# Four graph layers on one core: a shorter DMA tree for row sums, a work list planned with other landing times, and a rearranged head

## The chip, the cores and the metric

The kernel runs on one core of a Trainium2 chip. The metric is the device time of one execution in microseconds (us). Before the change the median of three runs is 1611.81 us (1611.36 to 1612.66).

The engines are named as the profile names them: PE is TensorE's matrix product and PEld its weight load, DVE is VectorE, ACT is ScalarE, POOL is GpSimd, SP is SyncE, which only issues DMAs here. Each engine runs its own list of instructions in order; semaphores hold an instruction until its operands are there.

## The reference

x has 32 graphs of 512 tokens and 128 features; adj is one 512 x 512 matrix of zeros and ones for all graphs. Four layers follow, each of the form x = x + layer(relu(layernorm(x))).

```python
# layer 0: attention-like, one score a[i, j] for each pair of tokens
x_h = elu(h @ Wi + bi)
e = sigmoid(a_tgt[:, :, None] + a_src[:, None, :] + be) * mask   # mask from adj
agg = einsum('bij,bjh->bih', e, x_h)
self_part = x_h * sum(e, axis=-1, keepdims=True)                 # the row sums of e
recv = elu(concat([agg, self_part]) @ Wn + bn)
out = concat([recv, x_h]) @ Wm + bm
# layer 1: five steps of a gated recurrent unit
av = concat([adj @ h, adj @ h])
z = sigmoid(av @ w3.T + ...); r = sigmoid(av @ w4.T + ...)
hv = tanh(av @ w5.T + r * h @ u5.T + ...); h = (1 - z) * h + z * hv
# layer 2: adj @ (h @ weight) + bias
# layer 3: sum over k of adj^k @ h @ weight_1[..., k], k up to 3
```

## The kernel before

**Tiles and number formats.** A graph is one tile of 128 partitions x 512. Graphs go in eight groups of four, since x tiles (kind x) and layer 3 take a group at once. Products with adj run in fp32r with each operand split into two parts, hi and lo (`parts`, line 948: a cast on ACT at L955, a subtraction on DVE at L959). The other products run in fp32. A branch on the values of adj chooses between two arms of the program; for this adj, which holds only zeros and ones, the arm `binary` runs. The branch is taken on the 1x1 tile `other`, which is the count of entries that are neither zero nor one (DVE at L567, four count matmuls at L596, a cast at L601, the branch at L1141).

**What sets the order.** The kernel first describes all its work as operations (`plan.op`), each with an engine, an assumed duration, a due time, its operands, and `result`, the assumed time from its end until others may use what it wrote. For a DMA that is the assumed landing time. A scheduler at build time (`Plan.order`) then walks through its own clock and, for each engine, takes the operation with the earliest turn whose operands are ready and whose buffers are free. What comes out is a fixed list for each engine. Due times are spread by `begin(b)`, 56 us a graph. `nudge` shifts the turns of chosen operations by random amounts from listed seeds: HEAD_NUDGES act on operations due in the first 130 us, TAIL_NUDGES on those due after TAIL. The plan is made up to HEAD (250 us) with the first list; the rest after that. Until 50 us the plan puts matmuls of `ones` with `ones` (L353) where PE would be idle; nothing uses their result.

**Layer 0's row sums.** The scores of a graph are four tiles `es`, one for each quarter of j, built by ACT (tanh, L729) and DVE (mask, L732). They go into PE's product with the messages (L741). Their sums over j come in different ways: for graphs 0 and 1 by matmuls with ones; for graphs 2 to 6 and 28 to 31 by sums of tiles and two fp32r matmuls (L784); and for the 21 graphs 7 to 27 by a tree of DMAs, `totals` (line 645). It works in DRAM tiles of kind m. SP copies es[0] to `half`; POOL's DMAs add es[1], es[2] and es[3] to it; another adds the lower half of its rows to the upper half; SP copies the first 32 of the remaining rows as strips into a small SBUF tile `few` (kind y, 128 x 128); POOL's DMA adds the other 32 to it. DVE transposes blocks of 32 (L659) and reduces (L660). `as_row` (L637, L640) sends the sums through DRAM (kind d) and reads them back as a row for all partitions (f<-d). DVE multiplies (own, L787), ACT puts the saved partial product back into PSUM (L792), and PE adds the product with Wn (L793).

**Other things that go by DMA.** `moved_blocks` and `turned`, `turned_back` transpose a tile by a DVE block transpose (L437), a write to DRAM (m<-f, L439) and a read (f<-m, L450, L469, or four reads at L474 where the order of layer 3 is wanted). The target scores also go through `as_row` from graph 4 on.

**Layer 1's step** is at lines 1000 to 1035: products with u3, adj, w4, w3, w5, u5 on PE (L496, L985), copies on ACT (L485), the sum in front of each gate on DVE (L1010), tanh on ACT (L501), r * h on DVE (L1017), which PE's product with u5 needs.

**The head.** SP and ACT issue the first loads: x of graph 0, then the four adj tiles on ACT's queue, x of graphs 1 to 3, then weights. PE transposes adj (L581), ACT casts it to fp32r (L589, L590). `layernorm` (line 519) takes moments on DVE (L528 to L531), the power -1/2 on POOL (L533), and then either scaling with relu on ACT (L542) or `normed` on DVE (L548, four pieces of 128 x 128; relu follows later, in the cast after the transpose). Behind the branch PE squares adj for layer 3 (L941, 16 matmuls, cast by ACT at L945), permutes its columns with `swap` (L973), and starts graphs 0 to 3.

Of the kernel before, what the change touches and what calls it, by code (L numbers as in the profile page):

```python
# [15 lines left out]
ALU = mybir.AluOpType  # L16
# [7 lines left out]
HEAD, TAIL = 250.0, 1500.0  # L24
HEAD_NUDGES = (7300007, 7300273, 7300133, 7300137, 7300212, 7300214, 7300262, 7300277, 35000194, 7300312, 7300318,
    7300325, 7300868, 7300483, 7300904, 7300717, 7300556, 7300600, 7300611, 7300613, 7300637,
    7300638, 7300675, 7300698, 35000259, 7300709, 7300722, 7300785, 35000013, 7300805, 35000212,
    7300852, 7300896, 35000078, 7300914, 7300921, 35000204, 35000148, 35000027, 35000249, 35000045,
    35000210, 35000052, 35000053, 35000077, 35000088, 35000089, 35000097, 35000105, 35000109,
    35000112, 35000115, 35000120, 35000122, 35000126, 35000131, 35000173, 35000144, 35000159,  # L30
    35000196, 35000203, 35000206, 35000211, 35000219, 35000232, 35000236, 35000250, 35000254,
    35000255, 35000256, 35000257, 35000258, 35000264)
TAIL_NUDGES = ()
# [220 lines left out]
def tile_four_graph_layers(  # L254
# [36 lines left out]
    BRANCH, FILL = 9.0, 50.0  # L291
    MARGIN = 10.0
    FIRST = 4
# [4 lines left out]
    A_LANDS = (2.9, 3.15, 3.4, 3.65)  # L298
# [4 lines left out]
    slots = {"x": 5, "f": 36, "q": 4, "s": 10, "d": 6, "y": 3, "m": 10, "b": 8}  # L303
# [9 lines left out]
    def buffers(pool, kind, n, shape, dt=F32):  # L313
# [7 lines left out]
        "y": buffers(pool, "y", slots["y"], [P, P]),  # L321
# [67 lines left out]
    load_graph(0, -10, 2.45)  # L389
    A_nat = [Val("f") for _ in range(NC)]  # L390
    for ic, v in enumerate(A_nat):
        load(v, adj.rearrange("(p c) n -> c p n", c=NC)[ic], -9.5, 0.45, earliest=0.3, result=A_LANDS[ic], eng="ACT")
    load_graph(1, -8.5, 2.9, 3.0)
    Wi_sb = load_const(Wi, [P, P], "Wi_sb", -8.2, earliest=3.0, result=2.7)
    load_graph(2, -8, 2.9, 3.0)
    load_graph(3, -7.5, 3.1, 3.0)
# [38 lines left out]
    def moved_blocks(src, due, us, view_out, view_in):  # L435
        blocks, moved = Val("f"), Val("m")
        op("DVE", us, due, lambda: nc.vector.transpose(view_out(at(blocks)), view_in(at(src))),  # L437
           [src], [blocks])
        op("SP", T_DMA, due, lambda: nc.sync.dma_start(at(moved), at(blocks)),  # L439
           [blocks], [moved], result=2.6)  # L440
        return moved
# [19 lines left out]
    def turned_back(src, due, in_order=False):  # L461
# [15 lines left out]
        op("SP", (4 if in_order else 1) * T_DMA, due, carry, [moved], [t], result=3.8)  # L477
# [41 lines left out]
    def layernorm(b, due, relu=True, earliest=0.0):  # L519
# [26 lines left out]
        def normed():  # L546
            for c in range(NC):
                nc.vector.tensor_scalar(  # L548
                    at(h)[:, ts(c, P)], at(X[b])[:, c, :], mean()[:, c : c + 1],
                    stat(SCALE)[:, c : c + 1], op0=ALU.subtract, op1=ALU.mult)  # L550
        if relu:
            op("ACT", 1.56, due, scale, [X[b], s], [h])
        else:
            op("DVE", 1.03, due, normed, [X[b], s], [h])
# [9 lines left out]
    n_odd = const("n_odd", [P, NC])  # L564
    for ic in range(NC):
# [3 lines left out]
            op0=ALU.is_gt, op1=ALU.not_equal, accum_out=at(n_odd)[:, ic : ic + 1]),  # L569
            [A_nat[ic]], [odd, n_odd], two=True)  # L570
# [23 lines left out]
    def count():  # L594
        for jc in range(NC):
            nc.tensor.matmul(  # L596
                at(p_odd)[:1, :1], at(n_odd)[:, jc : jc + 1], at(ones)[:, :1],
                start=jc == 0, stop=jc == NC - 1,
            )
    op("PE", 0.3, -1, count, [n_odd, ones], [p_odd])  # L600
# [30 lines left out]
    def as_row(columns, part, d, keep):  # L631
# [10 lines left out]
        op("SP", T_DMA, d, read, [row], [t], keep=keep, result=5.0)  # L642
        return t

    def totals(es, d):

        half, few, turned_few, columns = Val("m"), Val("y"), Val("y"), Val("s")
        def strip(k):
            return at(half)[ts(k, 32), :].rearrange("j (q i) -> q j i", q=4)
        def added(to, of, val):  # L650
            op("POOL", 1.0, d, lambda: nc.gpsimd.dma_start(to(), of(), accum_op=ALU.add),
               [*val, val[-1]], [val[-1]], two=False, result=4.6)
        op("SP", T_DMA, d, lambda: nc.sync.dma_start(at(half), at(es[0])), [es[0]], [half], result=2.6)
        for e in es[1:]:
            added(lambda: at(half), lambda e=e: at(e), [e, half])
        added(lambda: at(half)[: P // 2, :], lambda: at(half)[P // 2 :, :], [half])
        op("SP", T_DMA, d, lambda: nc.sync.dma_start(at(few), strip(0)), [half], [few], result=2.6)
        added(lambda: at(few), lambda: strip(1), [half, few])
        op("DVE", 0.25, d, lambda: nc.vector.transpose(at(turned_few), at(few)), [few], [turned_few])  # L659
        op("DVE", 0.25, d, lambda: nc.vector.tensor_reduce(  # L660
            at(columns)[:, :NC], at(turned_few).rearrange("p (b j) -> p b j", j=32),
            axis=mybir.AxisListType.X, op=ALU.add), [turned_few], [columns])
# [56 lines left out]
    def aggregated(b, begun, due):  # L719
# [43 lines left out]
        else:  # L763
# [13 lines left out]
            high, low, ps = Val("q"), Val("q"), Val("b")  # L777
# [36 lines left out]
    def entry(b):  # L814
        h = layernorm(b, begin(b), relu=b >= FIRST, earliest=begin(b) - 12.0 if b < G else 0.0)
# [17 lines left out]
    def arm(binary):  # L833
        with ExitStack() as stack:
# [15 lines left out]
            order = plan.order(end=HEAD)  # L850
# [3 lines left out]
    def list_rest(binary, pool):  # L854
        for v in crossing:
# [19 lines left out]
        for b in range(G):  # L875
            aggregated(b, begun[b], begin(b))

        n = 20 if binary else 16
        places["r"] = buffers(pool, "r", n, [P, 512], F32R if binary else F32)
        plan.free["r"] = [(0.0, i) for i in range(n)]  # L880
        PARTS = 2 if binary else 1
# [304 lines left out]
```

## Time and profile before

| what | value |
| --- | --- |
| median of 3 runs | 1611.81 us |
| the profiled execution | 1614.92 us |
| its span, first to last instruction | 1613.1 us |
| mean granted PE clock | 0.999 |
| PE busy | 1594.4 us (99%) |
| DVE busy | 1407.0 us (87%) |
| ACT busy | 1134.0 us (70%) |
| POOL busy | 282.5 us (18%) |
| mean share of the 16 DMA engines | 35.2% (q1, from SP and ACT), 12.3% (q0, from POOL) |
| landing f<-d, median | 5.6 us |
| landing m<-f from SP, from POOL | 2.4 us, 4.3 us |
| landing y<-m from POOL | 4.7 us |

A line of the views gives engine, source line, operation, and the tiles as written<-read with buffer numbers left out. In the view of waits, a line names the waiting instruction, then what released it, the sum of idle time, how often, and the longest. In a timeline, the first number is the start in us, the second the length of the merged piece, and what stands in brackets is the engine's idle time before it and what ended it. The span of the profiled execution is 1.8 us below its own time, and that time is 3.1 us above the median of the runs.

One fp32 matmul has two records in the profile, one fp32r matmul has one.

### The profile page before, as it was taken

To read this page: it belongs to the slowest core of one execution; us is meant where nothing else is said; L and a number is where in the kernel's file an instruction comes from. 1 tells how busy PE (TensorE), PEld (TensorE's weight loads), DVE (VectorE), ACT (ScalarE), POOL (GpSimd) and SP (SyncE) were. 2 spreads that over 40 slices of the span, in tenths; PEclk is the share of its full clock that TensorE was granted. 3 is DMA by queue.
4 is the path that set the end of the run, shared out by engine and by line. 5 is a ranking of instruction groups with operands and counts; after the bars stand their busy time and mean duration, and the time that the engine had idled before them with its cause. 6 is when DMAs were issued, how large, how long until landed. Compare 5 with 4: busy or idle time off the path is not lost. (4 is left out here: it accounts for less than half of the span.)

```text
span 1613.1 us, 21201 instructions
## 1 busy us (share of the span) xinstructions
PE 1594.4 (99%) x6285; PEld 1017.6 (63%) x6285; DVE 1407.0 (87%) x3356; ACT 1134.0 (70%) x2146; POOL 282.5 (18%) x286
## 2 busy tenths in 40 slices
PE   9999999999999999999999999999999999999998
PEld 6655555656666566666566665665666665656688
DVE  8899999989988899888989889888998888888772
ACT  7877767877776777766767678767787767666561
POOL 4121112202221122111122111221211111100010
PEclk9999999999999999999999999999999999999999
DMA  4364544554564555555555554555555344423221
GB/s 129 79 152 123 143 133 127 131 137 113 142 147 115 142 142 138 126 134 132 132 136 133 149 127 124 146 137 130 149 135 128 98 132 122 113 79 92 85 60 55
DMA packets 301281, 199.46 MB, mean 124 GB/s; under 512 B 89492, under 2 KB 249876, under 8 KB 300820
## 3 DMA queue, kind: packets, MB, share of 16 engines
q1 hardware_dynamic: 274708, 169.16, 35.2%
q0 software_dynamic: 24288, 27.01, 12.3%
q10 hardware_dynamic: 2160, 1.84, 0.3%
q8 instruction: 52, 0.85, 0.2%
q14 instruction: 73, 0.60, 0.1%
HBM read 93.79 MB, written 98.45 MB: 119 GB/s over the span
## 5 line engine op out<-in xcount | busy, mean ns | idle before, releaser
L485 ACT COPY f<-b 128x512 f32<-128x512 f32 x409 | 234.8, 584 | 157.8 <-PE b L985 109.1
L985 PE MATMUL b<-AQ,r 128*128 128x512 f32 x1024 | 303.9, 439 | 0.0
L533 POOL TENSOR_TENSOR s<-s,nhalf 128x4 f32<-128x4 f32 x128 | 153.6, 1200 | 624.8 <-DVE s L531 564.1
L985 PEld LDWEIGHTS b<-AQ,r 128*128 128x128 f32 x1024 | 192.4, 188 | 89.5 <-issue 43.6
L1010 DVE TENSOR_TENSOR f<-f,b 128x512 f32<-128x512 f32 x320 | 212.7, 677 | 33.0 <-PE b L496 26.2
L985 PE MATMUL b<-adj_r,r 128*128 128x512 f32 x768 | 225.4, 436 | 0.0
L437 DVE STREAM_TRANSPOSE f<-f 128x512 f32<-128x512 f32 x246 | 207.0, 846 | 18.7 <-ACT f L542 17.5
L542 ACT ACTIVATE f<-x,s 128x128 f32<-128x128 f32 x496 | 203.9, 486 | 26.1 <-DVE s L537 25.6
L985 PEld LDWEIGHTS b<-adj_r,r 128*128 128x128 f32 x768 | 144.6, 189 | 62.0 <-issue 26.8
L501 ACT ACTIVATE f<-f,b4w 128x512 f32<-128x512 f32 x160 | 115.3, 721 | 89.8 <-DVE f L1010 89.2
L959 DVE TENSOR_TENSOR r<-f,r 128x512 fp32r<-128x512 f32 x224 | 152.1, 683 | 20.2 <-ACT r L955 19.1
L496 PE MATMUL b<-f,u5T 128*128 128x512 f32 x320 | 163.3, 594 | 3.7 <-DVE f L1017 3.6
L955 ACT CAST r<-f 128x512 fp32r<-128x512 f32 x224 | 137.2, 619 | 42.3 <-DMA f<-m 38.1
L496 PE MATMUL b<-f,w4T 128*128 128x512 f32 x320 | 163.4, 593 | 0.0
L496 PE MATMUL b<-f,w3T 128*128 128x512 f32 x320 | 163.0, 592 | 0.0
L496 PE MATMUL b<-f,u3T 128*128 128x512 f32 x320 | 162.9, 594 | 0.0
L496 PE MATMUL b<-f,w5T 128*128 128x512 f32 x320 | 162.7, 592 | 0.0
L501 ACT ACTIVATE f<-f,b3w 128x512 f32<-128x512 f32 x160 | 115.1, 720 | 40.3 <-DVE f L1010 39.4
L501 ACT ACTIVATE f<-b,b5w 128x512 f32<-128x512 f32 x160 | 109.3, 684 | 36.9 <-PE b L496 36.1
L1060 PEld LDWEIGHTS b<-V,f 128*128 128x128 f32 x1024 | 122.4, 192 | 15.7 <-issue 14.1
L1027 DVE TENSOR_TENSOR f<-f,f 128x512 f32<-128x512 f32 x160 | 108.6, 680 | 22.4 <-ACT f L501 20.1
L1060 PE MATMUL b<-V,f 128*128 128x128 f32 x1024 | 123.7, 275 | 0.0
(121 smaller groups left out, 2339.0 us busy)
## 6 DMA issues: line engine op xcount, KB each, us to landing
m<-f SPq DMA_DIRECT2D x267, 256.0 KB, 2.4
f<-m SPq DMA_DIRECT2D x186, 256.0 KB, 3.0
m<-f POOLq DMA_DIRECT2D x63, 256.0 KB, 4.3
f<-m SPq DMA_DIRECT2D x240, 64.0 KB, 2.4
f<-d SPq DMA_DIRECT2D x49, 256.0 KB, 5.6
x<-in_x_dram SPq DMA_DIRECT2D x32, 256.0 KB, 4.0
out_dram<-x SPq DMA_DIRECT2D x28, 256.0 KB, 2.6
f<-f POOLq DMA_DIRECT2D x24, 256.0 KB, 3.7
```

What stands on the lines that cost most here:

```text
L437: op("DVE", us, due, lambda: nc.vector.transpose(view_out(at(blocks)), view_in(at(src))), [src], [blocks])
L485: op("ACT", us, due, lambda: nc.scalar.copy(at(t), at(src)), [src], [t])
L496: nc.tensor.matmul(to, at(w), of, start=start, stop=stop)
L501: op("ACT", us, due, lambda: nc.scalar.activation(at(dst), at(src), AF.Tanh, bias=at(bias), scale=scale), [src, bias], [dst])
L533: op("POOL", 1.2, due, lambda: nc.gpsimd.tensor_tensor(stat(SCALE), stat(VAR), at(neg_half), op=ALU.pow), [s, neg_half], [s], two=False)
L542: nc.scalar.activation(at(h)[:, ts(c, P)], at(X[b])[:, c, :], AF.Relu, bias=stat(SHIFT)[:, c : c + 1], scale=stat(SCALE)[:, c : c + 1],)
L955: op("ACT", T_COPY, due, lambda: nc.scalar.copy(part(hi), whole()), [src], [hi], keep=1)
L959: op("DVE", T_VEC, due, lambda: nc.vector.tensor_tensor(part(lo), whole(), part(hi).bitcast(F32), op=ALU.subtract), [src, hi], [lo], two=two)
L985: nc.tensor.matmul(at(pa), at(part)[:, ts(jc, P)], view(at(columns[jc])), start=jc == n == 0, stop=jc == NC - 1 and n == PARTS - 1,)
L1010: op("DVE", T_VEC, d, lambda: nc.vector.tensor_tensor(at(s), at(u), at(pg), op=ALU.add), [u, pg], [s])
L1027: op("DVE", T_VEC, d, lambda c=c, h=h: nc.vector.tensor_tensor(at(c), at(c), at(h), op=ALU.subtract), [c, h], [c], two=True)
L1060: nc.tensor.matmul(at(pz)[:, ts(i, D)], at(t[i])[:, ts(ic, P)], at(V[k]), start=i == n == 0, stop=last and i == G - 1 and n == len(terms) - 1,
```

## The change

- `totals`: no addition of the lower half of the DRAM tile to its upper half. SP copies two strips of 32 rows side by side into `few` (now 128 x 256), POOL adds the other two strips, each with its own DMA. DVE transposes 256 columns and reduces over two axes.
- The plan's assumed times: landings m<-f 2.6 to 3.0, tree additions 4.6 to 5.4, row reads f<-d 5.0 to 5.6, four ordered reads on SP 1.8 to 2.6 in all, the first loads; new seeds in HEAD_NUDGES, one seed in TAIL_NUDGES, TAIL at 1430 with the plan stopped there once.
- Head: the adj tiles are due first and go to SP's and ACT's queues in turn; BRANCH is 8.0 instead of 9.0; each column of the count is a value of its own.
- Layernorm: `normed` on POOL for the first layernorm of graphs 1 to 3 and for layer 1's layernorm of graphs 0 to 2, which had relu scaling on ACT. Relu of the latter moves into `parts` and into the copy after the transpose. Graph 2's first transposed h of layer 1 comes from PE instead of by DMA.
- The casts in `parts` are `activation` with Copy or Relu instead of `copy`.
- Buffers: f 39 instead of 36; in the arm `binary` the kinds r and q share 16 + 4 places instead of 20 and 4. POOL's folding of layer 3's weights starts at 60 us of the plan at the earliest.

The diff without its seeds:

```diff
-    BRANCH, FILL = 9.0, 50.0
+    BRANCH, FILL = 8.0, 50.0
-    FIRST = 4
+    FIRST, LATER, TURNED = 4, 1, 3
-    A_LANDS = (2.9, 3.15, 3.4, 3.65)
+    A_LANDS = (3.27, 2.75, 3.92, 3.55)
-    slots = {"x": 5, "f": 36, "q": 4, "s": 10, "d": 6, "y": 3, "m": 10, "b": 8}
+    slots = {"x": 5, "f": 39, "q": 4, "s": 10, "d": 6, "y": 3, "m": 10, "b": 8}
...
-        load(v, adj.rearrange("(p c) n -> c p n", c=NC)[ic], -9.5, 0.45, earliest=0.3, result=A_LANDS[ic], eng="ACT")
-    load_graph(1, -8.5, 2.9, 3.0)
+        load(v, adj.rearrange("(p c) n -> c p n", c=NC)[ic], -9.95, 0.45, earliest=0.3 * (ic % 2),
+             result=A_LANDS[ic], eng=("SP", "ACT")[ic % 2])
+    load_graph(1, -8.5, 4.25)
...
-           [blocks], [moved], result=2.6)
+           [blocks], [moved], result=3.0)
...
-        op("SP", (4 if in_order else 1) * T_DMA, due, carry, [moved], [t], result=3.8)
+        op("SP", 2.6 if in_order else T_DMA, due, carry, [moved], [t], result=3.8)
...
-                nc.vector.tensor_scalar(
+                (nc.gpsimd if by_pool else nc.vector).tensor_scalar(
...
+        elif by_pool:
+            op("POOL", 1.1, due, normed, [X[b], s], [h], two=False)
...
-        op("SP", T_DMA, d, read, [row], [t], keep=keep, result=5.0)
+        op("SP", T_DMA, d, read, [row], [t], keep=keep, result=5.6)
...
-        half, few, turned_few, columns = Val("m"), Val("y"), Val("y"), Val("s")
-        def strip(k):
-            return at(half)[ts(k, 32), :].rearrange("j (q i) -> q j i", q=4)
-        def added(to, of, val):
-            op("POOL", 1.0, d, lambda: nc.gpsimd.dma_start(to(), of(), accum_op=ALU.add),
-               [*val, val[-1]], [val[-1]], two=False, result=4.6)
-        op("SP", T_DMA, d, lambda: nc.sync.dma_start(at(half), at(es[0])), [es[0]], [half], result=2.6)
+        whole, few, turned_few, columns = Val("m"), Val("y"), Val("y"), Val("s")
+        def strips(k, start):
+            for n in range(2):
+                start(at(few)[:, ts(n, P)],
+                      at(whole)[ts(2 * k + n, 32), :].rearrange("j (q i) -> q j i", q=4))
+        def add(to, of):
+            nc.gpsimd.dma_start(to, of, accum_op=ALU.add)
+        op("SP", T_DMA, d, lambda: nc.sync.dma_start(at(whole), at(es[0])), [es[0]], [whole], result=3.0)
         for e in es[1:]:
-            added(lambda: at(half), lambda e=e: at(e), [e, half])
-        added(lambda: at(half)[: P // 2, :], lambda: at(half)[P // 2 :, :], [half])
-        op("SP", T_DMA, d, lambda: nc.sync.dma_start(at(few), strip(0)), [half], [few], result=2.6)
-        added(lambda: at(few), lambda: strip(1), [half, few])
...
+            op("POOL", 1.0, d, lambda e=e: add(at(whole), at(e)), [e, whole], [whole],
+               two=False, result=5.4)
+        op("SP", 1.2, d, lambda: strips(0, nc.sync.dma_start), [whole], [few], result=3.2)
+        op("POOL", 2.3, d, lambda: strips(1, add), [whole, few], [few], two=False, result=5.4)
+        op("DVE", 0.37, d, lambda: nc.vector.transpose(at(turned_few), at(few)), [few], [turned_few])
+        op("DVE", 0.35, d, lambda: nc.vector.tensor_reduce(
+            at(columns)[:, :NC], at(turned_few).rearrange("p (n b j) -> p b n j", n=2, j=32),
+            axis=mybir.AxisListType.XY, op=ALU.add), [turned_few], [columns])
...
-            order = plan.order(end=HEAD)
+            order = [*plan.order(end=HEAD), *plan.order(end=TAIL)]
             plan.nudge(TAIL, 2000.0, TAIL_NUDGES)
...
-            op("ACT", T_COPY, due, lambda: nc.scalar.copy(part(hi), whole()), [src], [hi],
-               keep=1)
+            op("ACT", T_COPY, due, lambda: nc.scalar.activation(
+                part(hi), whole(), AF.Relu if relu else AF.Copy), [src], [hi], keep=1)
...
-            tok = parts(h, due, two=True)
-            if b < 2:
+            tok = parts(h, due, two=True, relu=b < TURNED)
+            if b < TURNED:
...
-                layer1(b, layernorm(b, t), t + 6, G * PACE / STEPS)
+                layer1(b, layernorm(b, t, relu=b >= TURNED, by_pool=b < TURNED), t + 6, G * PACE / STEPS)
```

## The prediction, made before the changed kernel was run

> **What bounds the kernel now.** I read the page's busy shares first, then the chain that ended last, then the busy time by stretch, then what TensorE waited for, then the stretch around its dearest wait.
>
> ```profile
> span 1613.1 us, 21201 instructions
> PE 1594.4 (99%) x6285; PEld 1017.6 (63%) x6285; DVE 1407.0 (87%) x3356; ACT 1134.0 (70%) x2146; POOL 282.5 (18%) x286
> ...
> PE 31%; DVE 0%; issue 0%
> ```
>
> TensorE is the bound, and the chain's last 31% is TensorE alone. Only its 18.7 us of idle time, and matmuls that do nothing, can be won. By stretch (the columns are busy time of PE, PEld, DVE, ACT, POOL, then the granted clock, the DMA share and GB/s):
>
> ```profile
> 0.00:10.00 10.00, 7.65 (x42) 6.72 (x42) 4.88 (x22) 4.91 (x9) 2.54 (x10) 1.00 0.71 243
> 10.00:50.00 40.00, 39.91 (x218) 29.08 (x218) 38.39 (x127) 34.06 (x73) 17.56 (x27) 1.00 0.32 96
> 200.00:1104.00 904.00, 893.11 (x3408) 560.02 (x3407) 809.11 (x1938) 652.83 (x1239) 171.32 (x161) 1.00 0.53 133
> 1104.00:1608.00 504.00, 503.20 (x2111) 334.78 (x2110) 415.17 (x967) 328.14 (x617) 66.98 (x64) 1.00 0.40 106
> 1608.00:1613.20 5.20, 0.56 (x3) 0.14 (x1) 0.69 (x1) 0.00 (x0) 0.00 (x0) 0.97 0.39 110
> 335.00:340.00 5.00, 5.00 (x11) 3.14 (x12) 5.00 (x12) 3.54 (x8) 0.00 (x0) 0.66 0.63 144
> ```
>
> Idle: 2.35 us in the first 10, 0.09 up to 50, 10.89 from 200 to 1104, 0.80 from there to 1608 (all at 1108.65), 4.5 after the last matmul. From 1109 on TensorE never waits. The last row shows a second price: right after one wait the granted clock is 0.66 for 5 us, so 0.34 x 5 = 1.7 us more are lost.
>
> ```profile
> PE b L793 <- ACT b L792: 4.7, 3, 2.2
> PE b L496 <- DVE f L1017: 3.6, 3, 2.1
> PE b L741 <- DVE f L732: 2.4, 2, 1.7
> PE b L802 <- DVE f L621: 0.8, 1, 0.8
> ```
>
> So nine waits make the middle's 11.5 us. Their names are those of the last link; the timeline ahead of each shows where it began. The dearest:
>
> ```profile
> 325.77 1.19 POOL L651 DMA_DIRECT2D y<-m  x1 [3.17 <-DMA y<-m]
> ...
> 332.67 0.31 DVE L659 STREAM_TRANSPOSE y<-y 128x128 f32<-128x128 f32 x1 [3.34 <-DMA y<-m]
> 333.67 0.68 DVE L1010 TENSOR_TENSOR f<-f,b 128x512 f32<-128x512 f32 x1
> 334.26 0.68 DVE L1017 SCALAR_TENSOR_TENSOR f<-f,f 128x512 f32<-128x512 f32 x1
> 335.00 1.13 PE L496 MATMUL b<-f,u5T 128*128 128x512 f32 x2 [2.08 <-DVE f L1017]
> ```
>
> The tree's last added strip, issued at 325.77, landed 6.9 us later; the plan had counted 4.6 (result=4.6 in totals). DVE runs its list in order, so the gate of another graph stood behind the transpose for 3.34 us and TensorE behind that gate for 2.08. Reading the other eight the same way: 805.6 (2.24 us; ACT's cast L955 stood 3.01 us for a landing f<-m, with L792 behind it), 654.2 (1.26), 708.6 (1.70), 1103.3 (0.66) and 509.7 (0.14) (ACT's L729 stood 2.19, 2.63, 2.00 and 1.38 us for f<-d: planned 5.0, median landing 5.6). With 335.0 these are 8.1 us of late landings. The other waits, at 536.4 (0.64), 550.8 (0.92), 998.1 (1.18) and 1108.7 (0.78), are 3.5 us of queueing on ACT and DVE with no landing in it.
>
> **The change, part by part.**
>
> *Landing times in the plan.* as_row 5.0 to 5.6 us, m<-f 2.6 to 3.0, the tree's adds 4.6 to 5.4 on 63 whole tiles (median landing 4.3), four carries on SP 1.8 to 2.6 (the trace has 2.55 at 334.31). These run nothing themselves; they move consumers later in ACT's and DVE's lists. They speak to the 8.1 us, and to the 1.7 us of clock behind the dearest. TensorE has other graphs' work to put there, as its 99% shows. Value: -9.8; between 0 (a new order has as many misses) and -13.2 (all nine waits and the clock).
>
> [...] The row: 2.08 us idle at 335 and half speed for about 3.4 us after it (1.7 us lost); 2.24 us idle at 805.6 and none (805 to 810 has 1.00). [...] The row decides: 9.8, and a new wait of 2 us can cost 3.8.
>
> *The shorter tree, 21 times.* Before, one after another: SP copy (m<-f landings: 2.4), three POOL adds (3 x 4.3), half onto half (3.3), SP strip, strip add (4.7). After: the half step falls out, SP sends two strips (+0.56 issue) and POOL adds two (+1.16 issue), so 3.3 - 0.56 - 1.16 = 1.6 us shorter; DVE's transpose of 256 columns lies between 0.30 (128 columns, L659) and 0.70 (512, L437), say 0.43, and the reduction goes from 0.28 to about 0.42: +0.3 a tree, 6 us on an engine with 206 us free. The number of POOL adds in the trees stays 105, and POOL is 18% busy. All of this lies beside TensorE's work: own waits for the tree, due 52 us on. Value 0; if the cover goes, DVE's in-order wait is the cost (third rival below).
>
> *Adjacency first.* Five 256 KB tiles (x of graph 0 and four of adj) are now issued by 1.64 us, ahead of the other x tiles. Before, the last adj tile landed at 8.43, as the seventh of 1.90 MB with Wi: 0.92 MB at 184 GB/s in the first 5 us and 0.98 at about 300 in the next 3.3 (these two rates are the windows 0:5 and 5:10). As the fifth it comes after 1.31 MB: 5 + 0.39/0.30 = 6.3. Then the last is_gt check (0.69) 7.0, four count matmuls (0.34) 7.4; DVE has put the moments of graph 0 (1.36) in between, so the 1x1 cast ends at 8.5, TensorE's seven filling matmuls at about 9.0, and the branch at 9.0 to 9.9 (before: cast 10.54, first matmul behind the branch 11.87). bi_half now stands ahead of graph 0's pow on POOL and waits for bi_sb, which lands at 9.2 as before (the same 2.2 MB are ahead of it): pow ends 10.6, normed 11.7. TensorE has 13 squares (3.3 us) ahead of the transpose that needs it, so that is hidden; without this cover it costs up to 1.6.
>
> *Filling matmuls.* The listed order has 37 of them before and 29 after, 0.223 us each (74 records). Behind the branch 19 become 13: -1.3. TensorE's time up to 50 us that is no work for the result: before 11.87 - 2.5 (16 + 4 transposes of 0.11, the count) + 19 x 0.223 = 13.6; after 9.5 - 2.0 + 13 x 0.223 = 10.4. That is -3.2; I take off 0.7 for what follows: -2.5, between -3.5 and 0.
>
> *Layernorms on POOL.* Graphs 1 to 3's first and graphs 0 to 2's second. [...] The nearest rows, POOL's mask 128x512 at 0.62 and its 128x128 cast at 0.29, give 4 x 0.3 = 1.2 us (planned 1.1). [...] Graph 1's normed then ends near 16.0, the swap cast (0.89) at 16.9, and TensorE wants them at about 16 and 16.4: 0.5 to 1 us lost (the 0.7 above). DVE gets 12 of 16 pieces less; ACT loses three scalings of 1.66 us. A DVE normed beside a POOL mask took 1.77 instead of 1.11 (13.64), so the cover is thin in the head, and thick after it.
>
> *Graph 2 turned by TensorE*: four transposes more, 0.44 us. *activation(Copy) for copy* in 256 casts: the nearest row, ACTIVATE without a table bias (L627, 0.605), stands beside COPY (0.584), so 0; upper end +0.1 each by L501's 0.72, 26 us on an engine with 480 us free. *Buffers*: f 36 to 39, but the parts' r and q 24 to 20 together; value 0, cost unknown up to a few short waits. *The tail planned anew from 1430*: it had no wait, so it can only stay or lose; value 0.
>
> Sum against the profiled execution (1614.9, 1.8 more than its span): -9.8 - 2.5 + 0.4 = -11.9, so 1603.0. The median of the runs is 3.1 below the profiled one: 1600.
>
> **Rivals.** (1) *The head wins, the middle half*: every instruction is placed anew, and half of the saved 9.8 returns as new waits of the queueing kind: 1611.8 - 2.5 - 4.9 + 0.4 = 1605. For it: 3.5 us of such waits had no landing in them. (2) *It does not do what it says*: longer planned landings only shift waits, and four parts buffers fewer add some: 9.8 comes back, 1610 to 1612. For it: DVE at 87% has little room. Against it: 50 to 200 us ran without any wait. (3) *Slower, at the tree's last step*: two accumulating strips together, on one queue, could land later than the 7.7 us planned from the first issue (2.3 + 5.4). By the medians 1.16 + 4.7 = 5.9; by the worst seen 1.16 + 6.9 = 8.1. DVE then stands at the transpose in all 21 trees. The wait of 3.34 us cost TensorE 2.08, so 1.26 is covered; to eat 12 us, each tree must lose 0.57, that is land 9.5 us after the first issue. At 10.0: 21 x 1.04 = 22, so 1622.
>
> **Numbers.** 1600, likeliest, 0.50 (1596 to 1605); 1605 0.24 (up to 1608.5); 1611 0.13; 1622 0.13. A measurement of this kernel can tell about 0.2%, 3.2 us, from no change: faster 0.74, same 0.13, slower 0.13. Below 1594.5 everything must have gone, the nine waits too; the range reaches up to 1612.
>
> **What would show it.** Right: first matmul of the squares at 9 to 10; last adj landing near 6.3; TensorE's idle time from 200 to 1104 at 2 to 5 us instead of 10.9, no stretch of half clock behind it; DVE's waits for y<-m (12.2 us in 7 before) nearly gone; none from 1430 on. Wrong: waits for bi_sb, swap or a POOL normed in the first 20 us; DVE waits for y<-m in most trees; new PE waits for DVE L1010 or ACT's casts; gaps in the tail.

## The result and the profile after

The median of 14 runs after the change is 1612.2 us (1606.97 to 1614.19), that of 14 runs of the kernel before on the same chip 1611.44 (1608.54 to 1615.33). The ratio is 1.0002, interval 0.9991 to 1.0013: no difference that this measurement can tell. Forecast was 1600.0. The profiled execution took 1614.13 us; that of before 1614.92. In one version below (before with new landings and no seeds), one of four executions was slow, at 3927 us, and its ratio leaves it out.

The page of the kernel after, busy times:

```profile
span 1612.1 us, 21149 instructions
...
PE 1594.2 (99%) x6273; PEld 1017.9 (63%) x6273; DVE 1406.5 (87%) x3340; ACT 1131.2 (70%) x2135; POOL 311.4 (19%) x310
```

PE's sum is that of before, and its useful work is larger by only 0.4 us: what has changed is where PE is busy. The same view by stretch as before (busy PE, PEld, DVE, ACT, POOL, granted clock, DMA share, GB/s):

```profile
10.00:50.00 40.00, 37.41 (x174) 26.03 (x173) 33.13 (x107) 31.33 (x66) 25.16 (x32) 0.96 0.29 85
26.00:30.00 4.00, 4.00 (x23) 3.41 (x22) 1.88 (x4) 2.91 (x8) 4.00 (x5) 0.73 0.00 0
50.00:200.00 150.00, 147.35 (x512) 85.86 (x511) 133.38 (x297) 107.80 (x197) 42.33 (x44) 0.99 0.42 113
60.00:64.00 4.00, 4.00 (x9) 1.77 (x7) 3.96 (x15) 1.86 (x4) 0.57 (x1) 0.71 0.38 66
200.00:1104.00 904.00, 901.60 (x3447) 566.55 (x3446) 823.93 (x1959) 660.70 (x1253) 174.53 (x164) 1.00 0.55 136
1104.00:1608.00 504.00, 500.36 (x2097) 332.33 (x2095) 411.39 (x962) 325.74 (x611) 68.20 (x63) 1.00 0.39 105
```

From 200 to 1104 PE now idles 2.40 us instead of 10.89. But from 10 to 200 it idles 5.24 instead of 0.09, and the clock falls twice to half (24.7 to 28.2 and 58.9 to 62.3). From 1104 on it waits 2.90 us instead of 0.80; the other 0.74 us of the last row lie behind the last matmul, which ends at 1607.25. Of before, the one stretch not shown yet:

```profile
50.00:200.00 150.00, 150.00 (x510) 86.87 (x509) 138.82 (x305) 114.04 (x214) 24.08 (x24) 1.00 0.47 124
```

What PE waited for (waiting instruction, releaser, sum, times, longest):

```profile
PE b L437 <- POOL f L560: 4.5, 8, 1.2
PE b L810 <- ACT b L809: 1.9, 2, 1.7
PE b L597 <- DMA f<-in_adj_dram: 1.5, 1, 1.5
PE b L758 <- DVE f L749: 1.3, 1, 1.3
...
PE b L508 <- DMA f<-m: 1.0, 1, 1.0
```

L560 is `normed` (L548 before): the greatest wait is for the layernorm moved to GpSimd. DVE's wait for the tree is gone, in the view of waits of DVE, before and after:

```profile
DVE y L659 <- DMA y<-m: 12.2, 7, 3.5
...
DVE y L676 <- DMA y<-m: 0.3, 1, 0.3
```

**Work done by a time.** Busy time hides filling matmuls and half clock. So I add up the matmuls whose result is used, each with its mean spacing in the trace (fp32 with 512 columns 0.86 us, fp32r 0.23, 128 columns 0.22), up to some times. "2nd" is a second execution of before, told below. Each row is one execution.

| us of work done by | 12 | 50 | 200 | 1104 | 1600 | at the end |
| --- | --- | --- | --- | --- | --- | --- |
| before | 2.5 | 34.9 | 184.9 | 1072.9 | 1567.1 | 1575.5 |
| before, 2nd | 2.5 | 34.9 | 184.5 | 1076.3 | 1571.0 | 1575.5 |
| after | 3.4 | 33.1 | 177.5 | 1077.0 | 1568.9 | 1575.9 |

So after is 0.9 us ahead at 12, 7.4 behind at 200, gains 11.5 up to 1104 (7.7 against the second execution), and loses 2.3 (2.8) behind that.

**The pieces on GpSimd.** The line of `normed` (count, then ns: minimum, median, maximum):

```profile
L560 POOL TENSOR_SCALAR f<-x,s x24: 785/814/2314, 14.9 to 78.4; 128x128 f32<-128x128 f32 x24
L560 DVE TENSOR_SCALAR f<-x,s x4: 339/401/676, 11.3 to 12.5; 128x128 f32<-128x128 f32 x4
```

A piece takes GpSimd 0.79 us with nothing beside it, VectorE 0.34. A layernorm of four took GpSimd 3.2 us at best; planned was 1.1, forecast 1.2. (VectorE's four take 1.1, since its pieces overlap.) The long ones stand here (timeline: start, length, idle before in brackets):

```profile
28.28 2.59 DVE L749 SCALAR_TENSOR_TENSOR f<-f,mask 128x512 f32<-128x512 f32 x4 [1.93 <-ACT f L746]
28.37 5.96 POOL L560 TENSOR_SCALAR f<-x,s 128x128 f32<-128x128 f32 x4
```

The first piece of these four lasted 2.31 us, the second 1.90, both nearly all the time beside DVE instructions that read two tiles (L749, L775, L635). Of the 24 pieces, the eleven with no such neighbour lie at 0.79 to 0.82, the thirteen beside one at 0.79 to 2.31, five of them at 1.90 or more. PE's timeline shows the bill, with the four transposes that need those pieces one by one:

```profile
55.62 0.27 PE L437 MATMUL b<-ident,f 128*128 128x128 f32 x1
56.36 0.33 PE L437 MATMUL b<-ident,f 128*128 128x128 f32 x1 [0.46 <-POOL f L560]
57.73 0.33 PE L437 MATMUL b<-ident,f 128*128 128x128 f32 x1 [1.05 <-POOL f L560]
58.51 0.33 PE L437 MATMUL b<-ident,f 128*128 128x128 f32 x1 [0.45 <-POOL f L560]
```

1.96 us in three waits, and at 58.9 the clock goes to half. The transposes stand in PE's fixed list, and everything behind them waits as well.

### The profile page after: what moved, and what is told of

It is laid out like the page before. It is cut to its first block, busy times and chain, and to the rows that moved or that the text cites. A ratio compares the mean times of both kernels' runs of the same rounds, so it can differ in the third digit from the quotient of the medians.

```text
span 1612.1 us, 21149 instructions
## 1 busy us (share of the span) xinstructions
PE 1594.2 (99%) x6273; PEld 1017.9 (63%) x6273; DVE 1406.5 (87%) x3340; ACT 1131.2 (70%) x2135; POOL 311.4 (19%) x310
## 4 chain that ended last, share of the span: by engine, by line
PE 83%; DVE 6%; DMA 5%; ACT 2%; issue 2%; POOL 1%; SPq 0%; DVEq 0%; ACTq 0%; POOLq 0%
PE b L508 38%; PE b L1013 22%; PE b L1088 6%; PE b L758 6%; PE b L1097 3%; PE b L819 3%; DMA m<-f 2%; PE b L1076 2%; DMA f<-d 2%; PE b L810 2%; PE b L700 1%; DMA f<-m 1%; DVE f L449 1%; POOL f L560 1%; DVE s L540 1%
## 5 line engine op out<-in xcount | busy, mean ns | idle before, releaser
L545 POOL TENSOR_TENSOR s<-s,nhalf 128x4 f32<-128x4 f32 x128 | 149.1, 1165 | 725.3 <-DVE s L543 668.0
L1013 PE MATMUL b<-AQ,r 128*128 128x512 f32 x864 | 270.9, 436 | 0.0
L1013 PEld LDWEIGHTS b<-AQ,r 128*128 128x128 f32 x864 | 162.5, 188 | 75.9 <-issue 37.6
L554 ACT ACTIVATE f<-x,s 128x128 f32<-128x128 f32 x484 | 198.8, 487 | 15.5 <-DVE s L549 14.9
L1013 PE MATMUL b<-adj_r,r 128*128 128x512 f32 x600 | 188.1, 424 | 0.0
L978 ACT ACTIVATE r<-f 128x512 fp32r<-128x512 f32 x200 | 123.8, 628 | 28.4 <-DMA f<-m 22.6
L1013 PEld LDWEIGHTS b<-adj_r,r 128*128 128x128 f32 x600 | 111.9, 188 | 44.8 <-issue 17.2
L758 PE MATMUL b<-f,f 128*128 128x512 f32 x256 | 118.6, 600 | 1.3 <-DVE f L749 1.3
```

Source lines behind the costliest of these rows:

```text
L545: op("POOL", 1.2, due, lambda: nc.gpsimd.tensor_tensor(stat(SCALE), stat(VAR), at(neg_half), op=ALU.pow), [s, neg_half], [s], two=False)
L554: nc.scalar.activation(at(h)[:, ts(c, P)], at(X[b])[:, c, :], AF.Relu, bias=stat(SHIFT)[:, c : c + 1], scale=stat(SCALE)[:, c : c + 1],)
L758: op("PE", T_MM, d, lambda jc=jc, pn=pn: nc.tensor.matmul(at(pn), at(msg)[:, ts(jc, P)], at(es[jc]), start=jc == 0, stop=tree and jc == NC ...
L978: op("ACT", T_COPY, due, lambda: nc.scalar.activation(part(hi), whole(), AF.Relu if relu else AF.Copy), [src], [hi], keep=1)
L1013: nc.tensor.matmul(at(pa), at(part)[:, ts(jc, P)], view(at(columns[jc])), start=jc == n == 0, stop=jc == NC - 1 and n == PARTS - 1,)
```

## The experiments

Theory A: the middle gained as forecast, and `normed` on GpSimd, three times as long as planned, gave it back in the head. The rivals are named in the expectations. All ratios are to the kernel before on the same chip. The runs are from several chips, on which the median of before was 1608.55 to 1612.09 us, so versions of different groups are compared by ratio. "Idle" is PE's idle time in the profiled execution.

**Same list, pieces on VectorE.**

```diff
-                (nc.gpsimd if by_pool else nc.vector).tensor_scalar(
+                nc.vector.tensor_scalar(
```

> The lists of all engines stay those of the changed kernel; only the engine that runs the 24 pieces of normed is VectorE again, at the same places in the order. Theory A (the slow pieces on GpSimd cost the head its gain): TensorE's 4.5 us of waits ahead of the transposes that read normed go, the two half-clock stretches behind them (2 x 1.7 us) go, and the time falls by 6 to 8 us, to 1604 to 1606. Rival B (the head was lost to the new order itself, and VectorE, with 24 pieces of about 0.28 us more in 80 us, becomes the one that is waited for): other waits take their place, 1610 to 1612.

Measured: 1607.38 us, ratio 0.9970 (0.9961 to 0.9980).

```profile
10.00:50.00 40.00, 38.77 (x187) 26.38 (x186) 37.52 (x129) 33.54 (x71) 11.85 (x20) 1.00 0.30 84
50.00:200.00 150.00, 149.70 (x524) 87.57 (x523) 140.74 (x310) 109.07 (x198) 29.73 (x33) 1.00 0.45 119
```

With no instruction moved in any list, idle time from 10 to 200 falls from 5.24 to 1.53, no half clock is left, and the waits for `normed` are gone. So GpSimd's pieces hold 5.2 us by the ratios (4.8 by the medians), less than the 6 to 8 expected, and this is not yet the forecast. Part of the rest belongs to this one execution. The record of the granted clock begins with its first rise, at 10.23 us here and at 4.26 in the profile of the kernel after (the view's clock reads 1.00 from 0 to 10 in both). PE's 16 transposes of adj, here and in the kernel after:

```profile
6.10 3.66 PE L597 MATMUL b<-ident,f 128*128 128x128 f32 x16 [0.85 <-DMA f<-in_adj_dram]
...
6.32 2.25 PE L597 MATMUL b<-ident,f 128*128 128x128 f32 x16 [1.47 <-DMA f<-in_adj_dram]
```

Most of these records last 0.42 us here and 0.28 there, and the squares begin at 11.66 instead of 10.35.

**The plan is told the true time.**

```diff
-            op("POOL", 1.1, due, normed, [X[b], s], [h], two=False)
+            op("POOL", 3.6, due, normed, [X[b], s], [h], two=False)
```

> The pieces stay on GpSimd, but the plan counts 3.6 us for the four instead of 1.1, so that everything is listed anew. Theory A: TensorE finds other work while they run, its waits for them fall below 1 us, and the time falls to 1604 to 1608, if the new order is no worse elsewhere (up to 3 us either way, by the draw). Rival B: no gain, 1610 to 1613.

Measured: 1615.3, ratio 1.0018 (1.0010 to 1.0026). No PE matmul waits for L560 any more, and the half clock is gone, but the listed order has 52 filling matmuls in place of 29: 23 x 0.223 = 5.1 us. With this order, the delay is only filled, not spared. Neither theory had expected a time this long.

**Planned anew for VectorE.**

```diff
-            op("POOL", 1.1, due, normed, [X[b], s], [h], two=False)
+            op("DVE", 1.03, due, normed, [X[b], s], [h])
```

(and the pieces issued on VectorE.)

> The pieces go to VectorE in the plan too (1.03 us counted), everything is listed anew. Theory A: as with the same lists, 1603 to 1608, and TensorE idle under 1.5 us between 10 and 200 us. Rival B: VectorE at over 80% in the first 80 us can't take 6.7 us more, TensorE waits for it instead, 1610 to 1613.

Measured: 1607.19, ratio 0.9971 (0.9961 to 0.9982); 48 filling matmuls. No better than the same list with the pieces on VectorE.

**Constants in place of the two scalars of each partition.**

```diff
-                    at(h)[:, ts(c, P)], at(X[b])[:, c, :], mean()[:, c : c + 1],
-                    stat(SCALE)[:, c : c + 1], op0=ALU.subtract, op1=ALU.mult)
+                    at(h)[:, ts(c, P)], at(X[b])[:, c, :], 0.0, 1.0,
+                    op0=ALU.subtract, op1=ALU.mult)
```

> The changed kernel's lists; the 24 pieces on GpSimd take the constants 0 and 1 in place of the two per-partition scalars, so that these layernorms only copy x (the subtraction of the mean and the scaling are left out for the first layernorm of graphs 1 to 3 and layer 1's of graphs 0 to 2). Theory P (a piece is slow because of its per-partition scalars): a piece alone falls from 0.79 us to about 0.3, TensorE's waits for them from 4.5 us to under 1.5, and the time to 1605 to 1608. Rival S (it is slow because it shares access with VectorE, or has this price whatever its scalars are): the shortest piece stays over 0.6 us, the longest over 1.8, and the time stays at 1610 to 1613.

Measured: 1604.61, ratio 0.9969 (0.9954 to 0.9984).

```profile
L561 POOL TENSOR_SCALAR f<-x x24: 632/718/1007, 14.7 to 68.8; 128x128 f32<-128x128 f32 x24
```

The mean and the scale are left out here, and the order of all instructions is that of the kernel after. Alone a piece falls only from 0.79 to 0.63, but beside DVE's two-tile instructions it stays at 0.65 to 1.01, where the kernel after had up to 2.31. So the operands read from SBUF for each partition make up most of the long ones, though not most of the price of a piece alone: each theory is right in one half. At 200 us this list has done 186.9 us of work, 2.0 more than before: with a `normed` of about 2.9 us on GpSimd, the forecast gain of the head is there.

**Landing times taken back.** The kernel after with 2.6, 5.0, 4.6 and 1.8 us for its landings:

```diff
-           [blocks], [moved], result=3.0)
+           [blocks], [moved], result=2.6)
...
-        op("SP", T_DMA, d, read, [row], [t], keep=keep, result=5.6)
+        op("SP", T_DMA, d, read, [row], [t], keep=keep, result=5.0)
...
-        op("POOL", 2.3, d, lambda: strips(1, add), [whole, few], [few], two=False, result=5.4)
+        op("POOL", 2.3, d, lambda: strips(1, add), [whole, few], [few], two=False, result=4.6)
```

> The changed kernel with the landing times that the plan had before (m<-f 2.6, rows 5.0, tree additions 4.6, strips 2.6, four ordered reads 1.8); the tree stays short, and the list up to about 60 us stays the same. Theory A (the landing times made the middle better): TensorE's idle time from 200 to 1104 us rises from 2.4 to 8 or more, with waits behind landings of y, f<-d and f<-m, and the time rises to 1617 to 1621. Rival C (the middle got better by the shorter tree or by the draw of a new order): idle time stays under 5 us, 1611 to 1614.

Measured: 1629.43, ratio 1.0116 (1.0097 to 1.0136), idle 9.61 from 200 to 1104. In the view of waits:

```profile
ACT r L978 <- DMA f<-m: 50.7, 38, 4.3
...
PE b L810 <- ACT b L809: 6.2, 5, 2.5
```

In the kernel after it was:

```profile
ACT r L978 <- DMA f<-m: 22.6, 18, 3.9
```

ACT stood 28 us longer for f<-m; behind it is PE's wait of L810, 1.9 us in the kernel after. The size was more than expected (1617 to 1621): idle time and one half clock in the middle make about 9 us of the 17, the rest is not accounted for. Everything was also placed anew.

**The kernel before with the new landing times, and with the tree as well.** (The edit above the other way round; in the second, `totals` of after, with `few` 256 wide and 19 r buffers instead of 20.)

> The kernel before, with nothing changed but the landing times in the plan (m<-f 3.0, rows 5.6, tree additions 5.4, strips 3.2, four ordered reads 2.6); long tree, old loads, layernorms on VectorE and ScalarE. Theory A (these times alone make the middle better): TensorE idle from 200 to 1104 us falls from 10.9 to 4 or less, and the time from 1611 to 1601 to 1605. Rival C (it takes the shorter tree or the 39 f buffers): idle stays above 7, 1608 to 1612.

> The kernel before with the same landing times and with the shorter tree (and 19 r buffers instead of 20, which its wider strip tile makes necessary). Theory A: the tree lies beside TensorE's work, so the time is within 2.5 us of that with the long tree and the same landing times. Rival C: the shorter tree is what helps, at least 4 us less than with the long tree.

Measured: 1611.04, ratio 1.0008 (0.9999 to 1.0017), and 1606.81, ratio 0.9984 (0.9975 to 0.9993). The middle, landing times alone and then with the tree:

```profile
200.00:1104.00 904.00, 897.02 (x3437) 565.37 (x3436) 802.44 (x1926) 652.50 (x1235) 175.28 (x164) 1.00 0.55 133
```

```profile
200.00:1104.00 904.00, 902.94 (x3474) 570.30 (x3473) 822.14 (x1965) 662.40 (x1256) 180.89 (x166) 1.00 0.55 136
```

Idle 6.98 against 1.06. The landing times alone brought nothing; the forecast had put the tree at nothing and the landing times at everything. Together they brought 0.16%, 2.6 us (3.9 by the medians), without any change in the head.

**Loads as before, on the version planned for VectorE.**

```diff
-        load(v, adj.rearrange("(p c) n -> c p n", c=NC)[ic], -9.95, 0.45, earliest=0.3 * (ic % 2),
-             result=A_LANDS[ic], eng=("SP", "ACT")[ic % 2])
+        load(v, adj.rearrange("(p c) n -> c p n", c=NC)[ic], -9.5, 0.45, earliest=0.3,
+             result=A_LANDS[ic], eng="ACT")
```

> The changed kernel listed anew with normed on VectorE, and with the loads of before (adj on ScalarE's queue alone, x of graphs 1 to 3 and Wi between, BRANCH 9.0). As predicted for the loads (branch 1.5 to 2.5 us earlier): this takes 1.5 to 3 us more than the same kernel with the new loads, 1609 to 1610. Rival (the head is a chain through graph 0 that the earlier branch doesn't shorten): within 1.5 us of it, 1606 to 1608.5.

Measured: 1609.21, ratio 0.9990 (0.9977 to 1.0002), against 0.9971 of its twin. But idle in the middle was 5.42 against 2.30, and at 200 us this list had done 0.7 us more work than its twin, not less. So the difference can't be put down to the loads, and no run shows what the new loads are worth.

**Relu of layer 1 back on ACT, on the version planned for VectorE.**

```diff
-                layer1(b, layernorm(b, t, relu=b >= TURNED, by_pool=b < TURNED), t + 6, G * PACE / STEPS)
+                layer1(b, layernorm(b, t), t + 6, G * PACE / STEPS)
```

> The changed kernel without its layernorm part: normed of graphs 1 to 3 on VectorE, layer 1's layernorm of graphs 0 to 2 scaled with relu by ScalarE as before, listed anew. Theory A (only the pieces on GpSimd cost the head; loads, landing times and tree are worth keeping): 1603 to 1608, TensorE idle from 10 to 200 us under 2. Rival B (the head of the changed order is worse by itself): 1609 to 1612.

Measured: 1609.94, ratio 1.0001 (0.9993 to 1.0010). PE idles little in the head (1.14 us from 50 to 200), but the list has 48 filling matmuls and at 130 us has done 110.8 us of work against 115.1 before. A list without waits can be slow by itself. That pointed to the seeds.

**Seeds of the head left out,** in seven versions.

```diff
-HEAD_NUDGES = (7300035, 7300086, 7300060, 7300091, 7300132, 7300189, 7300254, 7300923, 7300554, 7300610, 7300478,
...
+HEAD_NUDGES = ()
```

> The changed kernel with the old landing times in the plan and without the seeds that shift turns in the head: another draw of the order. Theory A (old landing times leave consumers too early in the lists): TensorE idle from 200 to 1104 us is 8 or more again. Rival D (the first draw was bad luck): under 5.

> The kernel before with the new landing times and the long tree, without the seeds in the head: another draw. Theory E (both are needed: the landing times and the shorter tree, since with the long tree idle was 7.0): idle from 200 to 1104 us between 5 and 10. Rival A (the landing times alone do it, and the first draw was unlucky): under 4.

> The changed kernel listed anew with normed on VectorE, without the seeds in the head: another draw with the new landing times. Theory A: TensorE idle from 200 to 1104 us is 1 to 5 (2.3 with the seeds); the head is some us worse, since nothing was searched for it, 1608 to 1614. Rival D (the middle is a matter of the draw): idle above 7.

> The kernel after with HEAD_NUDGES = (), planned anew; normed of six layernorms stays on GpSimd. Theory A (the time of normed on GpSimd ate the gain of the middle): still late pieces and TensorE waits for them in the first 130 us, so 1605 to 1610, 4 us or more above the version with normed on VectorE and no seeds (1601.3). Theory S (the seeds are the harm: they were picked for a plan whose list does not hold on the chip): 1600 to 1604, with TensorE idle for less than 1 us between 10 and 200 us, although the pieces on GpSimd take as long as before.

> The same lists as the kernel after without seeds, the pieces of normed issued on VectorE in place of GpSimd. Theory A: faster than its twin on GpSimd by 4 to 6 us, as with the seeds (4.9), near 1601 to 1605. Theory S: within 2 us of its twin.

> The plan is told 3.6 us for a normed on GpSimd instead of 1.1, without seeds. Theory A: telling the plan does not give the time back, since what stands behind normed is late in the plan too: 1606 to 1612. Theory S: without the seeds a plan that knows the time loses little, 1601 to 1605.

> The kernel before with HEAD_NUDGES = (). Theory A says nothing of it but that seeds chosen for a plan with true times should help: 1612 to 1616, slower than with them. Theory S in its wide form (seeds do harm or nothing): 1608 to 1612. TensorE's idle time from 200 to 1104 stays 8 to 13 us in both, since the landing times are the old ones.

Measured, as ratios to before (the intervals are those without seeds), with the filling matmuls and the work done by 200 us. The work is that of one execution each, and a late first rise of the clock, as in the same list on VectorE (10.23 us) and in the kernel after without seeds (9.94), lets the squares begin 1.3 to 1.6 us later.

| list | ratio, seeds | ratio, none | fillers, seeds / none | work by 200, seeds / none |
| --- | --- | --- | --- | --- |
| before | 1 | 1.0040 (1.0030 to 1.0049) | 37 / 62 | 184.9 / 178.0 |
| after | 1.0002 | 1.0003 (0.9993 to 1.0013) | 29 / 48 | 177.5 / 178.0 |
| after, same list on VectorE | 0.9970 | 0.9998 (0.9987 to 1.0008) | 29 / 48 | 183.1 / 178.9 |
| told 3.6 us | 1.0018 | 0.9978 (0.9970 to 0.9987) | 52 / 52 | 178.8 / 181.3 |
| planned for VectorE | 0.9971 | 0.9946 (0.9927 to 0.9964) | 48 / 41 | 180.6 / 185.1 |
| before, new landings | 1.0008 | 1.0073 (1.0050 to 1.0096) | 37 / 61 | 184.7 / 178.3 |
| after, old landings | 1.0116 | 1.0040 (1.0024 to 1.0056) | 29 / 48 | 180.6 / 177.8 |

The seeds of before spare it 25 filling matmuls (5.6 us) and are worth 0.4%. Those of after spare 19 (4.2 us) in its plan. With the pieces on VectorE the same list keeps this on the chip (183.1 against 178.9 us of work by 200); on GpSimd nothing of it is left (177.5 against 178.0). In versions with other durations than the seeds were listed with they do harm: clearly with told 3.6 and old landings, while for planned for VectorE the two intervals just touch. Before with new landings still needs its own. So theory S, that the seeds are the harm, fell: after without them is no faster. Theory A stands for the list as it is, and with less weight without seeds: 1609.78 on GpSimd against 1607.81 on VectorE, 2.0 us by the medians, with ratios whose intervals overlap. And against A, a plan that knows the 3.6 us and has no seeds loses little: 1605.44. What costs is less GpSimd's time itself than a tight list that does not know of it.

The version planned for VectorE without seeds is the fastest of all, 1601.33 us (1600.84 to 1603.18, four runs), and beats both kernels. Its head has neither waits nor half clock:

```profile
10.00:50.00 40.00, 40.00 (x199) 27.91 (x198) 38.39 (x125) 32.43 (x68) 13.33 (x20) 1.00 0.29 83
50.00:200.00 150.00, 149.99 (x532) 88.31 (x530) 141.02 (x313) 110.91 (x204) 27.14 (x30) 1.00 0.46 124
200.00:1104.00 904.00, 902.40 (x3468) 569.04 (x3467) 823.41 (x1973) 660.68 (x1254) 185.13 (x168) 1.00 0.55 136
```

**Before, and before without seeds, profiled a second time,** nothing edited.

> The kernel before, unchanged, profiled a second time. Theory M (its waits between 200 and 1104 us come from its list and the landing times it was planned with): TensorE's idle time there is 7 to 12 us again, at mostly the same places (335, 654, 709, 805, 998). Theory L (landings differ from run to run, and so do the waits): a good part of the places is different, and the sum is anything from 3 to 12 us, in step with the run's time.

> The kernel before without seeds, profiled a second time; its first profile had 0.25 us of idle time between 200 and 1104 us with the old landing times and the long tree, but was its fastest run, 5.8 us under its median. Theory M: this list has no such waits, so again under 2 us, and the 5.8 us are elsewhere. Theory L: if the run is near the median (1615.7), 4 to 6 us of waits stand between 200 and 1104 us.

Measured: 1610.77 us and 1612.15 (one run each). The middle of before in its second execution:

```profile
200.00:1104.00 904.00, 896.51 (x3417) 562.15 (x3415) 812.48 (x1942) 656.74 (x1246) 171.35 (x162) 1.00 0.54 134
```

Idle 7.49 instead of 10.89. The waits at 654, 806, 998 and 1103 us are there again, each 4 to 6 us earlier (1.48, 2.48, 1.02 and 0.93 us). That at 335, the dearest with its half clock, is 0.32 instead of 2.08, and the 1.70 at 708.6 is gone. So most waits belong to the list, and some to the single execution. The half clock is there once in both, at 336.3 in the first and at 800.4 in the second. Before without seeds, in its two executions:

```profile
200.00:1104.00 904.00, 903.75 (x3470) 570.43 (x3469) 824.05 (x1982) 662.41 (x1258) 176.91 (x167) 1.00 0.55 137
```

```profile
200.00:1104.00 904.00, 901.56 (x3456) 567.62 (x3455) 822.54 (x1972) 662.14 (x1256) 175.89 (x166) 1.00 0.55 136
```

It idles only 0.25 and 2.44 us in the middle, with the old landing times and the long tree: they aren't needed for a middle without waits. Both executions (1609.93 and 1612.15) lie well below this version's median of 1615.7, and what its slower runs lose is not known. Over all lists: new landings with the short tree idle 1.06 to 5.42 us there (twelve profiles, median 2.5); the six versions that lack one or both idle 0.25 to 10.89, and five of these always over 6.

## Why the forecast was wrong, step by step

The terms of the forecast's sum, each against what was measured:

- **Layernorms on POOL: the step that failed.** It put 1.2 us on a layernorm, from POOL's mask and cast rows, and 0.7 us on what follows. Measured: 3.2 to 6.0 us a layernorm, PE waits of 4.5 us, 2 x 1.7 us of half clock. Alone, 3.2 us against VectorE's 1.1 is 2.9 times as long. Where it came up to 6, the five pieces of 1.90 to 2.31 us all stand beside VectorE instructions that read two tiles (L749 and L775 among them). But the pieces with constants read x from SBUF as well and stay at 1.01 or less beside such instructions. So the per-partition operands are what suffers most; why, no run tells. The prediction had such a meeting in hand, VectorE's normed of 1.77 instead of 1.11 us beside a GpSimd mask, and charged it to VectorE alone. The forecast had named the sign, "a POOL normed in the first 20 us"; one wait of 0.33 us came at 18.2, the others at 21.9 to 24.9 and at 56.4 to 58.5.
- **Head sum -2.5: wrong sign, +7.4 by the work done at 200 us.** 4.8 us are GpSimd's pieces by the same-list experiment (5.6 by the work done). Of the other 1.8 us, up to 1.3 are the late first rise of the clock in that one execution, which let the squares begin at 11.66 instead of 10.35 us; the rest stays open. Behind the pieces stands this: the shorter list (29 fillers, as forecast) was worth 2.0 us with the pieces of 0.72 us, and nothing with those of 0.79 to 2.31.
- **Adjacency first: half right.** The last adj tile landed by 6.2 (forecast 6.3). Then the tests of three tiles on DVE ran one after another, 6.21 to 8.05, not one of 0.69 us behind the last landing; the moments of graph 0 followed, and the cast ended at 9.45 (forecast 8.5), the squares began at 10.35 (9.0 to 9.9; before 11.87). Graph 0's pow ended at 11.06 and its normed at 12.85 (forecast 10.6 and 11.7); both were hidden, as forecast.
- **Middle -9.8: size right, cause half right.** 11.5 us came by the work done, 7.7 against the second execution. But the landing times alone brought nothing, the tree was counted at 0, and both together brought 2.6 to 3.9 us when nothing else changed. A list without them, but without the head's seeds, had hardly a wait there in two executions either. So that the size came so near is in part luck. The waits that were summed are ten, not the nine that the prediction says, as its own list shows; the sum stays.
- **From profile to median: counted twice, as far as one more execution shows.** The profiled execution of before lay 3.1 us above the median; its second execution, 4.2 us faster, had done 3.4 us more work by the middle's end, since the waits at 335 (2.08 to 0.32) and 708.6 (1.70) were all but absent. These microseconds were in the 9.8, and were taken off again with the 3.1.
- **Tail 0: wrong, 2.3 to 2.8 us lost,** in waits of 2.90 us at 1187 to 1240 us (among them 0.98 for a landing f<-m at 1227 and 1.26 for L749 at 1240). They lie before 1430; from 1241 on there is no wait, as forecast. The middle's new list doesn't end at 1104.
- **Right at their sizes:** the tree's transpose 0.436 (0.43) and reduction 0.409 us (0.42), DVE's waits for y<-m 12.2 to 0.3, so the third rival did not come; graph 2's transposes +0.44 us of work. A cast by `activation` took 0.63 us instead of 0.62. The buffers and the new plan of the tail were not tested alone. The lower end of the range, 1594.5, doesn't come out of the prediction's terms: 1611.8 - 13.2 - 3.5 + 0.4 = 1595.5.

Together, from the forecast for the profiled execution, 1603.0: head +9.9, tail +2.3, middle -1.7 make 1613.5, measured 1614.1. The profile of after lay 1.9 us above its median, not 3.1, which is the remaining 1.2 of the miss. The second rival had the right time, 1610 to 1612, with the wrong reason: the middle's time did not come back in the middle.

## What to carry to other kernels

An operation moved to another engine has to be priced from that engine with the same operands, per-partition scalars included, and with what runs beside it; a row of another form on the same engine was off nearly three times here. A fixed list that is packed tightly has no cover for a wrong duration: six durations, each too short by 2.1 to 4.9 us, cost 4.5 us of waits and 3.4 us of clock here, and what the seeds had gained in the plan was gone on the chip. Before the waits of one execution are summed, a second execution says which of them belong to the list, and the difference to the median must not be taken off twice.

## What the runs showed of the hardware

**When the clock halves.** In all traces the granted clock changes only at multiples of 3.413 us from its first rise: in the kernel after 20.48, 3.413, 30.72 and 3.413 us lie between changes, that is 6, 1, 9 and 1 stretches. Of some 9,300 such stretches in 20 profiles, up to the last matmul, 11 are followed by one at half clock: nine in which PE was busy 0.00 to 1.46 us, and two of 1.49 and 1.70. Six others of 1.48 to 1.63 are not (in five of them the last matmul ends), and all the rest were busy 1.73 us or more. So in these traces 1.46 or less always halved the clock, 1.73 or more never, and between them both happened. PE need not have idled through a whole stretch here: one with up to 1.46 us of work in its 3.41 was still followed by half clock. The two waits of before that the prediction set side by side differ by how they lie to the stretches: the 2.08 us at 335.0 lie whole in one (332.91 to 336.33, PE busy 1.33), and the next is at half clock; the 2.24 at 805.6 are split at 803.95, the stretch behind that point was busy 1.76, and the clock stayed at 1.00. By these two, a wait of a little over 2 us counts or not by where it falls; in the second execution the wait there was 2.48 and the clock halved at 800.4:

```profile
799.89 1.61 PE L793 MATMUL b<-f,Wn_sb 128*128 128x512 f32 x2 [2.48 <-ACT b L792]
```

In the kernel after, no single wait ahead of the two falls was longer than 1.2 us, but transposes of 0.3 us among waits for GpSimd made two stretches busy 1.35 and 1.46 us. Each cost about 1.7 us (half of 3.41). This was read off the traces, with no run made to test it.

**The first rise of the clock.** In the 20 profiles it comes between 3.86 and 10.23 us after the first instruction, and the list does not set it: one list had it at 4.26 with the pieces on GpSimd and at 10.23 with them on VectorE, another at 9.94 and at 3.86. With the late rise the squares of adj began 1.3 and 1.6 us later. So two profiled heads should be compared only after this is taken out.

**GpSimd beside VectorE.** 128 x 128 in fp32 with two per-partition scalars takes GpSimd 0.79 us alone and up to 2.31 beside two-tile VectorE instructions; with constants 0.63 alone and 1.01 at most.

**One execution.** Of one kernel, executions on one chip lay 9.4 us apart with no change in the list (before: 1604.68 to 1614.11 in 47 runs).
